# Bringing node columns by hand in a graph layer: 26 double groups on two queues, not 43 on three

## The chip, the core and the metric

The kernel runs on one core of a Trainium2 chip. The metric is device time in microseconds. Three runs of the kernel before took 5406.4, 5420.59 and 5431.38 us, so the median is 5420.59 us. A core has five engines that run side by side, each with its own queue of instructions in program order: TensorE (PE), VectorE (DVE), ScalarE (ACT), GpSimd (POOL) and SyncE (SP), which here only issues DMAs. Within a queue nothing overtakes.

## The reference, cut to what matters

There are 12,500 nodes of 128 features and 400,000 edges, sorted by their destination.

```python
h = jnp.maximum(_layernorm(x), 0.0)
s, d = (src, dst)
m = jax.nn.relu(jnp.concatenate([h[s], h[d], ea], -1) @ w1 + b1) @ w2 + b2
agg = jax.ops.segment_sum(m, d, num_segments=12500)
gi, gh = agg @ w_ih + b_ih, h @ w_hh + b_hh
# a GRU cell of gi, gh and h, added to x
```

Each edge needs a row that depends on its source node. Sources are random, so this row has to be fetched edge by edge; this fetch is what the change is about.

## The kernel before, in words

**Tables.** A first stage computes `h`, keeps it transposed in SBUF (`hT_all`, one column of 128 features for each node) and writes `A = h @ w1a`, one 512-byte row for each node, to DRAM.

**Groups and units.** The 3,125 tiles of 128 edges are cut into 391 double groups of eight tiles (`NP`, index `k`). Each double group is two units of 512 edges (`u = 2k + h`). A fully unrolled loop runs over the 782 units. For a unit, TensorE multiplies the destination part and the edge attributes with the weights (`pre`, L599), VectorE adds the source rows (`add`, L624), ScalarE applies the ReLU into `RB` (`relu`, L630), and TensorE sums the edges of each node (`seg`, L643). In program order, the round of unit `u` holds `pre(u+3)`, `add(u+2)`, `relu(u+2)` and `seg(u)`.

**Four ways to bring the source part of a double group:**

- *Gather* (most double groups): eight indirect DMAs on POOL (L147), each bringing 128 rows of `A` into a tile `G`. There are 7 such tiles (and 4 more at the start). The gathers of a double group wait until the ReLU of the double group that used the tile before is done.
- *ScalarE by hand* (19 double groups): 1,024 copies of one column each, `hT_all` to `HE_act` (L795). TensorE then multiplies the columns with `w1a` (L610), so no `A` row and no `add` is needed.
- *VectorE by hand* (18 double groups): the same with 1,024 reductions of one column (L797) into `HE_dve`.
- *SyncE by hand* (6 double groups): 1,024 plain DMAs of one 512-byte row of `A` into the tile `G_sp` (L802), of which there is one. `add` and `relu` then run as for a gathered double group.

By hand, each column's place is a register value. 32 values are loaded at a time from the tile `at` (L789).

**Which double groups, and when.** L85 to L94 spread each engine's double groups evenly over a range of `k`; for SP the range is 20 to 381. One job at a time runs on an engine. Its steps are dealt out evenly over the units between its start and its end, and they stand in the engine's queue between the ordinary work of these units:

```python
for m, kl in order.items():
    start = 2 * JOBS0
    for k in kl:
        end = 2 * k - (8 if m == "sp" else 4)
        jobs.setdefault(start, []).append((m, k, end - start))
        start = end if m != "sp" else 2 * k + 2
```

`JOBS0` is 15, so jobs start at unit 30. An SP job for double group `k` ends 8 units before it is used, and the next starts 2 units after, when `G_sp` is free.

**What else SP's queue holds.** For every four units it issues `Ld` (two DMAs, L495, destinations, three tiles) and `L` (L486, edge attributes, three tiles). `Ld` is issued 6 rounds and `L` 5 rounds before the round of its first use (`onehot_T` on DVE, L502, and `pre` on PE), and both wait for a tile to come free. For every 14 double groups it loads `xb` (L665) and stores `out` (L734).

Of the kernel before, what the change touches and what calls it, by code (L numbers as in the profile page):

```python
# [43 lines left out]
CH = PLACE * PAIR  # L44
LOAD = 32
STEP = {"act": 4, "dve": 4, "sp": 2}
SPREAD = {"dve": 18, "act": 19, "sp": 6}
NR = 12672

H_AT = 16512  # L50
# [6 lines left out]
def tile_gnn(ctx: ExitStack, tc: tile.TileContext, x, src, srcT, dstT, dstP, eaT, eaP, w1, b1, w2T, b2,  # L57
# [26 lines left out]

    mode, order = {}, {m: [] for m in SPREAD}  # L85
    for m, n in SPREAD.items():
        lo, hi = {"dve": (JOBS0 + 3, NP - 14), "act": (JOBS0 + 11, NP - 6),
# [1015 lines left out]
```

## Time and profile before

The profiled execution took 5395.6 us. Its span, first to last instruction, is 5393.5 us, so 2.1 us lie around it; it is 0.46% below the median of the three runs. In the table, a line is that of the code, "busy" counts time in instructions, and the idle time stands before the instructions of that row.

| Row of the profile | Count | Busy us | Mean of one, ns | Idle before, us |
| --- | --- | --- | --- | --- |
| L624 DVE add into G | 676 | 460.9 | 682 | 276.9 |
| L630 ACT ReLU, from G | 676 | 424.8 | 629 | 430.9 |
| L599 PE pre | 3128 | 1369.6 | 577 | 901.4 |
| L643 PE seg | 6250 | 716.4 | 371 | 0.8 |
| L610 PE on HE_dve | 288 | 56.2 | 330 | 0.1 |
| span | | 5393.5 | | |

No engine is busy for more than 58% of the span. Register loads, register moves and DMA issues are not counted as busy, and on ACT, DVE and SP these are many. The jobs run from 340 us (first row on SP at 339.9 us) to 5249 us on SP and 5342 us on ACT.

### The profile page before, as it was taken

To read this page: it belongs to the slowest core of one execution; us is meant where nothing else is said; L and a number is where in the kernel's file an instruction comes from. 1 tells how busy PE (TensorE), PEld (TensorE's weight loads), DVE (VectorE), ACT (ScalarE), POOL (GpSimd) and SP (SyncE) were. 2 spreads that over 40 slices of the span, in tenths; PEclk is the share of its full clock that TensorE was granted. 3 is DMA by queue.
4 is the path that set the end of the run, shared out by engine and by line. 5 is a ranking of instruction groups with operands and counts; after the bars stand their busy time and mean duration, and the time that the engine had idled before them with its cause. 6 is when DMAs were issued, how large, how long until landed. Compare 5 with 4: busy or idle time off the path is not lost. (4 is left out here: it accounts for less than half of the span.)

```text
span 5393.5 us, 95106 instructions
## 1 busy us (share of the span) xinstructions
PE 3101.8 (58%) x13578; PEld 1854.8 (34%) x13578; DVE 2712.7 (50%) x22515; ACT 2718.9 (50%) x20936; POOL 2654.9 (49%) x2789
## 2 busy tenths in 40 slices
PE   2664555556555556556655555665556565556557
PEld 2542333333333323333333333333333233333334
DVE  3645545545454545455545455545454555555453
ACT  2433345555555555555555555555555555555554
POOL 5445445544555454545454555544455544544452
PEclk7775665666566666666666666666666666666667
DMA  3322122222222222222221222222222222222221
GB/s 107 90 65 63 52 58 63 62 56 56 60 59 59 60 60 55 61 57 62 56 60 52 58 61 58 61 60 56 60 58 56 59 60 58 60 58 58 57 58 44
DMA packets 157887, 325.93 MB, mean 60 GB/s; under 512 B 65057, under 2 KB 77132, under 8 KB 157255
## 3 DMA queue, kind: packets, MB, share of 16 engines
q0 software_dynamic: 88992, 182.43, 13.1%
q1 hardware_dynamic: 68119, 137.33, 8.9%
q14 instruction: 520, 4.26, 0.3%
q8 instruction: 112, 1.84, 0.1%
q10 hardware_dynamic: 144, 0.07, 0.0%
HBM read 305.74 MB, written 13.84 MB: 59 GB/s over the span
## 5 line engine op out<-in xcount | busy, mean ns | idle before, releaser
L147 POOL DMA_INDIRECT G<-A,src_i x2704 | 2581.1, 955 | 2658.2 <-ACT RB L630 1766.9
L795 ACT COPY HE_act<-hT_all 128x4 uint8 x19456 | 2155.6, 189 | 1758.6 <-issue 1733.5
L797 DVE TENSOR_REDUCE HE_dve<-hT_all 128x4 uint8 x18432 | 1406.9, 146 | 1166.2 <-issue 1157.3
L599 PE MATMUL pre<-RW,L 128*128 128x256 f32 x3128 | 1369.6, 577 | 901.4 <-DVE G L624 748.7
L599 PEld LDWEIGHTS pre<-RW,L 128*128 128x128 f32 x3128 | 799.3, 282 | 1279.6 <-issue 651.5
L524 PE MATMUL oh<-w1b,hw 128*64 128x128 f32 x782 | 245.4, 412 | 1203.9 <-DVE hw L521 599.5
L643 PE MATMUL seg<-RB,OH 128*32 128x129 f32 x6250 | 716.4, 371 | 0.8 <-issue 0.8
L630 ACT ACTIVATE RB<-G 128x512 f32<-128x512 f32 x676 | 424.8, 629 | 430.9 <-issue 175.0
L533 DVE TENSOR_TENSOR RW<-oh,b1b 32x128 f32<-32x128 f32 x782 | 218.6, 279 | 773.5 <-issue 657.3
L624 DVE TENSOR_TENSOR G<-pre,G 128x512 f32<-128x512 f32 x676 | 460.9, 682 | 276.9 <-issue 269.0
L524 PEld LDWEIGHTS oh<-w1b,hw 128*64 128x64 f32 x782 | 103.6, 188 | 1416.5 <-DVE hw L521 705.7
L643 PEld LDWEIGHTS seg<-RB,OH 128*32 128x32 f32 x6250 | 382.6, 141 | 281.1 <-issue 184.8
L651 DVE COPY sums<-seg 64x128 f32<-64x128 f32 x391 | 107.4, 275 | 181.6 <-remote 94.6
L502 DVE TENSOR_SCALAR L<-Ld,node_of 64x512 f32<-64x512 int32 x391 | 192.3, 492 | 2.1 <-issue 1.6
L652 ACT CAST dcol<-seg 64x1 f16<-64x1 f32 x391 | 59.4, 152 | 232.4 <-DVE sums L651 146.0
L551 DVE TENSOR_TENSOR OH<-dloc,iota 128x256 f32<-128x256 f16 (+1 forms) x392 | 163.0, 416 | 15.2 <-issue 11.7
L674 PEld LDWEIGHTS nd<-spot,sums 64*128 64x128 f32 x782 | 160.6, 314 | 15.5 <-issue 15.5
L674 PE MATMUL nd<-spot,sums 64*128 64x40 f32 x782 | 164.6, 398 | 2.2 <-issue 2.2
L638 PE MATMUL seg<-zrow 1*64 1x129 bf16 x391 | 115.0, 294 | 0.0
L327 PE MATMUL pre<-w1a,hT_all 128*128 128x128 f32 x196 | 51.6, 414 | 77.2 <-remote 30.4
L693 PE MATMUL nd<-DEG,brow 33*128 33x512 f32 x112 | 89.4, 889 | 2.7 <-ACT RB L630 1.7
L697 PE MATMUL nd<-TOT,w2ih 128*128 128x512 f32 x112 | 87.8, 878 | 0.0
(151 smaller groups left out, 1625.5 us busy)
## 6 DMA issues: line engine op xcount, KB each, us to landing
G_sp<-A SPq DMA_DIRECT2D x6144, 0.5 KB
Ld<-in_dstP SPq DMA_DIRECT2D x390, 128.0 KB
L<-in_eaP SPq DMA_DIRECT2D x195, 256.0 KB
G<-A,src_i POOLq DMA_INDIRECT x2704
xb<-in_x SPq DMA_DIRECT2D x28, 256.0 KB
out<-xb SPq DMA_DIRECT2D x28, 256.0 KB
xs<-in_x SPq DMA_DIRECT2D x11, 512.0 KB
A<-asb SPq DMA_DIRECT2D x11, 512.0 KB
```

Source lines behind the costliest of these rows:

```text
L147: nc.gpsimd.indirect_dma_start(out=G[k][:, j, a, :], out_offset=None, in_=table, in_offset=bass.IndirectOffsetOnAxis(ap=src_i[c][:, i:i + ...
L502: nc.vector.tensor_scalar(Ls[k // QP][:2 * V, c], Ds[k // QP][:, c], node_of[:, k:k + 1], None, op0=ALU.is_equal)
L524: nc.tensor.matmul(PB_[k][:2 * V, :D], hw.rearrange("p a v -> p (a v)"), w1b, start=True, stop=True)
L533: nc.vector.tensor_tensor(RW[k % 4][s, a, :], pm[s, :D], b1b[s, :], op=ALU.add)
L551: nc.vector.tensor_tensor(o, d.to_broadcast(shape), i.to_broadcast(shape), op=ALU.is_equal)
L599: nc.tensor.matmul(PP[u][:, 2 * i:2 * i + 2, :], Ls[k // QP][:, c0:c0 + 128], RW[k % 4], start=True, stop=not raw)
L624: nc.vector.tensor_tensor(RT[u], PP.pop(u), RT[u], op=ALU.add)
L630: nc.scalar.activation(o[:, :, :D], RT.pop(u), AF.Relu)
L643: nc.tensor.matmul(SEG[k][V * a:V * (a + 1), :D + 1], OH[k][:, j, a, :], RB[u % 3][:, (j % 2) * 2 + a, :D + 1], start=False, stop=all(b != ...
L674: nc.tensor.matmul(pt[:, bass.ds(offs[i], V + SHIFT)], sums[:, i, :], spot, start=False, stop=i == n - 1)
L795: nc.scalar.copy(he[:, e * 4:e * 4 + 4], h_bytes[:, bass.ds(v - H_AT, 4)])
L797: nc.vector.tensor_reduce(he[:, e * 4:e * 4 + 4], h_bytes[:, bass.ds(v - H_AT, 4), None], AX.X, ALU.max)
```

## The change

One line: VectorE brings no columns, ScalarE brings 19 double groups as before, and SP brings 7 instead of 6.

```diff
 STEP = {"act": 4, "dve": 4, "sp": 2}
-SPREAD = {"dve": 18, "act": 19, "sp": 6}
+SPREAD = {"dve": 0, "act": 19, "sp": 7}
```

What follows from it in the queues: 18,432 reductions and their 576 register loads leave VectorE. 1,024 row DMAs and 32 register loads are added to SP, whose double groups are now 71, 123, 174, 226, 277, 329 and 381. The number of double groups that are gathered rises by 17, so POOL issues 2,840 gathers from `A` and not 2,704. For these 17 and the one on SP, VectorE's `add` takes the place of TensorE's products with `w1a` (L610). ScalarE's jobs stay as they are.

## The prediction

> **What bounds the kernel now.** I read the page's engine rows first. No engine is near full:
>
> ```profile
> PE 3101.8 (58%) x13578; PEld 1854.8 (34%) x13578; DVE 2712.7 (50%) x22515; ACT 2718.9 (50%) x20936; POOL 2654.9 (49%) x2789
> L147 POOL DMA_INDIRECT G<-A,src_i x2704 | 2581.1, 955 | 2658.2 <-ACT RB L630 1766.9
> L795 ACT COPY HE_act<-hT_all 128x4 uint8 x19456 | 2155.6, 189 | 1758.6 <-issue 1733.5
> L797 DVE TENSOR_REDUCE HE_dve<-hT_all 128x4 uint8 x18432 | 1406.9, 146 | 1166.2 <-issue 1157.3
> ```
>
> In the groups, POOL waits for ScalarE's ReLU (it frees `G`), and ScalarE and VectorE idle at "issue": their own queue is late. So I read timelines, start and length in us first. POOL in one cycle:
>
> ```profile
> 2517.96 0.94 POOL L147 DMA_INDIRECT G<-A,src_i  x1 [0.30 <-issue]
> 2519.21 0.94 POOL L147 DMA_INDIRECT G<-A,src_i  x1 [0.30 <-issue]
> 2520.45 0.94 POOL L147 DMA_INDIRECT G<-A,src_i  x1 [0.30 <-issue]
> 2524.74 0.94 POOL L147 DMA_INDIRECT G<-A,src_i  x1 [3.34 <-ACT RB L630]
> ```
>
> and ScalarE beside it:
>
> ```profile
> 2520.12 0.19 ACT L795 COPY HE_act<-hT_all 128x4 uint8 x1 [0.51 <-issue]
> 2520.83 0.19 ACT L795 COPY HE_act<-hT_all 128x4 uint8 x1 [0.52 <-issue]
> 2521.54 0.19 ACT L795 COPY HE_act<-hT_all 128x4 uint8 x1 [0.52 <-issue]
> 2522.26 0.19 ACT L795 COPY HE_act<-hT_all 128x4 uint8 x1 [0.52 <-issue]
> 2522.96 0.57 ACT L795 COPY HE_act<-hT_all 128x4 uint8 x5 [0.51 <-issue]
> ```
>
> Eight gathers follow each other at 1.25 us. In their later part ScalarE issues one column per 0.71 us; afterwards one per 0.095 us. SP's records step at the same moments, even for register moves. Over the 314 bursts of eight, ScalarE's spacing is 0.10 to 0.14 us in the first 4 us and 0.51 to 0.68 us from 7 to 11 us; it recovers 11.4 us after the burst's start. I call this the **crawl**. A cycle has a median of 14.4 us; it is crawl plus the work of the queues between crawls.
>
> Then I read SP. Its waits inside its fourth job (2876 to 3616 us; us in total, times, longest), and a piece of its timeline there:
>
> ```profile
> SPq L802 <- DMA G_sp<-A: 9.4, 20, 0.7
> SPq L802 <- DMA L<-in_eaP: 1.3, 2, 0.7
> SPq L103 <- DMA G<-A,src_i: 1.1, 1, 1.1
> ```
>
> ```profile
> 2909.68 0.83 SPq L495 DMA_DIRECT2D Ld<-in_dstP  x2
> 2910.61 0.48 SPq L486 DMA_DIRECT2D L<-in_eaP  x1
> 2911.19 14.45 SPq L802 DMA_DIRECT2D G_sp<-A  x20
> ```
>
> Against some 15 us of waits in 740 us, SP issues all the time. Twenty rows take 6.85 us outside the crawl and 14.45 us here. In this job SP loses three units against the ReLUs; in the other five it waits 23 to 81 us a job, mostly for `Ld` and `L` tiles to come free. Nobody waits for SP yet. SP is thus the queue that has no room left, and the change gives it 1,024 rows more.
>
> **The change, part by part.** Sums are made against the span of 5393.5 us.
>
> *VectorE's columns leave:* 18,432 reductions, 1406.9 us busy and 1157.3 us of issue idle, 2,564 us of its queue. What it can give is what others wait for VectorE: ScalarE's semaphore waits over 0.3 us sum to 705 us between 340 and 5340 us, half of it (276 of 560 us counted from 600 to 5000 us) in the 3 us after a crawl, where VectorE clears its columns ahead of `add`. I take at most 705 us, at least nothing, and nothing is taken unless ScalarE paces.
>
> *TensorE's L610 products:* 56 us busy, beside idle time: nothing. *36 more `add`s:* 36 x 0.682 = 25 us on VectorE, which has just lost 2,564: nothing.
>
> *17 more double groups gathered:* 136 x 1.25 = 170 us of POOL, which idles 2,658: nothing there. But 17 bursts more crawl. A double group without a burst passes in some 9 us, one with it in 14.4, so the crawl costs up to 17 x 5.4 = 92 us if everything stays on this cycle, and 0 if another queue paces that doesn't lose. Inside SP's sum it is counted below.
>
> Here the Trainium skill speaks against these rows: "SBUF — State Buffer" (SBUF: two separate sides) has engines and DMA disjoint, and only VectorE locking out GpSimd's descriptors. By it, 17 more bursts cost the other queues 0, and a silent VectorE could only speed the gathers up. The rows: a gather takes 944 ns in the median, and 945 on average in the prologue, where no column runs; and ScalarE's columns, which are no DMA, step at 0.71 us. I take the rows: no faster gather, and a crawl per burst.
>
> *SP's seventh double group.* "DMA: Bandwidth & Descriptors" (Issuing engines are not separate DMA queues) says that an issuer's time is usually small beside the DMA. By that rule this part costs about 0: DMA engines are at 22%. The row says the issue is the price: 0.323 us a row outside the crawl, 592/1024 = 0.578 us in job 4. A job now:
> - Job 4 took 741 us: 592 on rows, 149 on the rest (32 register loads at 2.1 us = 67; `L`, `Ld`, `xb`, `out` 82). Rows beyond 1024 x 0.323 = 331 are crawl: 261 us over 392 gathers, 0.666 us a gather. Jobs 2, 3, 5 and 6, waits taken off, come to 709 to 732 us; the mean of jobs 2 to 6 is 722.
> - After, jobs stand 51.6 double groups apart, so a job has 93 units of program, not 109: the rest falls by 12 us. SP may slip until 8 more ReLUs are done than its place in the program says: there PE stops at `pre` for `L`. It starts level with the ReLUs at 2k+2 and ends 2.5 units ahead of the next such point, so 100.7 of the 103.2 units of a period pass during the job, with 46.8 bursts or 374 gathers; 18 fewer x 0.666 = 12 us.
> - J = 741 - 24 = 717 us from job 4; 722 - 23 = 699 from the mean.
> - Would a silent VectorE loosen the crawl for SP? Sorting 274 bursts by VectorE's instructions in them, SP loses 58.6% of the burst in the fifth with 35 and 55.6% in that with 56: no. Around 5305 us, with SP and VectorE silent, ScalarE gets about two per step. Bounds 0 and 10% of 236 us; I take 2%, 5 us, the sorted row being nearer. J = 708 - 5 = 703 us.
>
> The other queues could pass the 103.2 units of a period in about 6.1 us each (6.81 now, less 0.96 of ScalarE's waits, plus the new bursts), 630 us, which J is above. So SP slips by its 8 units and then **sets the pace**: PE waits at `pre` for `L` (behind it stand `seg` and the next products, and ScalarE waits for them), or VectorE at L502 for `Ld` (behind it stands `add`). The DMA engines, 22% busy, don't notice 0.5 MB more.
>
> Sum: start 340; seven jobs 7J = 4921; the first has 11 units more, 32; six gaps of 2.5 units (`add`, ReLU, then `G_sp` is free), 6 x 16 = 96; from the last row, about ReLU 761, to the end 88 (the span's last 124 us after ReLU 754, less seven units at 5.2). 340 + 4921 + 32 + 96 + 88 = 5477 us, 84 us more than 5393.5. On the median of the runs, which is 27 us above the span, that is **5505 us.** J = 691 would be break-even: 0.541 us a row, against 0.553 in J = 703.
>
> **Rivals** (on the same basis).
> - *The crawl is shared more than I think.* Without VectorE, SP loses 10 to 15% less: J 667 to 693, 5250 to 5435. For it: the stretch at 5305 us; against it: the sorted bursts.
> - *ScalarE paces, faster.* VectorE was the late engine, seen in ScalarE's waits. 5393.5 - 705 + 17 bursts x 5 = 4774, on the median 4800, or 5150 if half of the waits stay. It decides only if SP keeps up at 630 us a period, 0.48 us a row; jobs 2 to 6 never went below 0.547.
> - *The gather cycle paces.* SP's slip stays covered and each double group keeps its 14.4 or 9 us: 5393.5 + 92 + 27 = 5513. Same side; it differs in that no `pre` waits for `L`.
> - *The change does less than it says*: excluded, the instruction lists have 2,840 gathers, 7,168 rows and no reduction.
>
> **Chances.** SP paces as summed, 5420 to 5600: 0.58. Shared crawl: 0.23. ScalarE paces: 0.07. Gather cycle: 0.08. Slower than 5600: 0.04. Of the first, 0.05 lies within 0.5% of the median (5393 to 5448, about what a measurement tells from no change) and 0.53 above; of the second 0.08 within, 0.15 faster. Faster 0.22, same 0.13, slower 0.65. The range leaves out ScalarE and the outermost of the others: 5300 to 5640. The likeliest alone: 5420 to 5600.
>
> **What would show it.** Right: SP issues in its jobs without waits, `L` and `Ld` come late (PE `pre` and DVE L502 wait for their DMA), ScalarE's wait turns from VectorE to those, POOL idles more. Wrong: SP still waits for tiles; rows of `G_sp` under 0.52 us; ScalarE without waits; bursts closer than 14 us.

## The result and the profile after

Five runs of the changed kernel took 5347.73 to 5369.74 us, median 5365.62; five of the kernel before took 5406.4 to 5431.38, median 5420.41. The ratio is 0.9898, 95% interval 0.9872 to 0.9925: 1.0% faster, where 1.6% slower was forecast. The profiled execution took 5347.73 us, its span is 5345.6 us.

The page's engine row and the groups that answer to those of before (busy us, mean ns of one, idle before, releaser of most of it):

```profile
PE 2754.2 (52%) x13290; PEld 1648.9 (31%) x13290; DVE 1475.8 (28%) x4119; ACT 2696.9 (50%) x20936; POOL 2781.1 (52%) x2925
L147 POOL DMA_INDIRECT G<-A,src_i x2840 | 2707.4, 953 | 2481.8 <-ACT RB L630 1524.6
L795 ACT COPY HE_act<-hT_all 128x4 uint8 x19456 | 2151.6, 189 | 1589.4 <-issue 1562.2
L599 PE MATMUL pre<-RW,L 128*128 128x256 f32 x3128 | 1226.0, 526 | 1663.6 <-DMA L<-in_eaP 1375.5
```

The last row is the one that changed its meaning. TensorE's `pre` used to wait for VectorE's `add` (748.7 us). It now waits 1375.5 us for `L`, a transfer that SP issues. SP's own waits inside its fourth job (2489 to 3171 us; total, times, longest) and a piece of its timeline there:

```profile
SPq L802 <- DMA G_sp<-A: 15.9, 31, 1.4
SPq L802 <- ACT RB L630: 9.7, 1, 9.7
SPq L486 <- PE oh L524: 0.4, 1, 0.4
```

```profile
2497.03 0.83 SPq L495 DMA_DIRECT2D Ld<-in_dstP  x2
2497.95 0.49 SPq L486 DMA_DIRECT2D L<-in_eaP  x1
2498.55 28.75 SPq L802 DMA_DIRECT2D G_sp<-A  x44
```

SP waits 26 us in 682 and issues without a pause; 44 rows with their register loads hold `L` and `Ld` back for 28.75 us. So SP sets the pace, as forecast. POOL and ScalarE in one cycle:

```profile
2517.72 0.94 POOL L147 DMA_INDIRECT G<-A,src_i  x1 [0.30 <-issue]
2518.97 0.94 POOL L147 DMA_INDIRECT G<-A,src_i  x1 [0.31 <-issue]
2530.86 0.94 POOL L147 DMA_INDIRECT G<-A,src_i  x1 [10.95 <-ACT RB L630]
```

```profile
2505.40 0.19 ACT L795 COPY HE_act<-hT_all 128x4 uint8 x1 [0.44 <-issue]
2506.11 0.29 ACT L795 COPY HE_act<-hT_all 128x4 uint8 x2 [0.52 <-issue]
2506.84 0.19 ACT L795 COPY HE_act<-hT_all 128x4 uint8 x1 [0.44 <-issue]
2507.55 0.29 ACT L795 COPY HE_act<-hT_all 128x4 uint8 x2 [0.51 <-issue]
```

The crawl's step is still 0.71 us, but before it carried one copy of ScalarE in the lines shown, and now it carries one or two. The forecast had no such change in it. The sum with the terms as they came out, from the starts of the instructions (us):

| Term | Forecast | Measured |
| --- | --- | --- |
| start | 340 | 343.7 |
| first job | 735 | 744.8 |
| six later jobs | 4218 (703 each) | 4075.5 (674 to 686, mean 679) |
| six gaps | 96 | 89.9 |
| last row to the end | 88 | 91.7 |
| span | 5477 | 5345.6 |

Four terms are off by 10 us or less. The later jobs are 142 us shorter than forecast, and the whole miss of the span is 131. A row took 0.535 us in the mean (0.531 to 0.540), where 0.553 stood in the forecast and 0.541 would have been break-even.

### The profile page after: what moved, and what is told of

It is laid out like the page before. It is cut to its first block, busy times and chain, and to the rows that moved or that the text cites. A ratio compares the mean times of both kernels' runs of the same rounds, so it can differ in the third digit from the quotient of the medians.

```text
span 5345.6 us, 77966 instructions
## 1 busy us (share of the span) xinstructions
PE 2754.2 (52%) x13290; PEld 1648.9 (31%) x13290; DVE 1475.8 (28%) x4119; ACT 2696.9 (50%) x20936; POOL 2781.1 (52%) x2925
## 5 line engine op out<-in xcount | busy, mean ns | idle before, releaser
L147 POOL DMA_INDIRECT G<-A,src_i x2840 | 2707.4, 953 | 2481.8 <-ACT RB L630 1524.6
L599 PE MATMUL pre<-RW,L 128*128 128x256 f32 x3128 | 1226.0, 526 | 1663.6 <-DMA L<-in_eaP 1375.5
L599 PEld LDWEIGHTS pre<-RW,L 128*128 128x128 f32 x3128 | 731.0, 258 | 2006.9 <-issue 1798.7
L643 PE MATMUL seg<-RB,OH 128*32 128x129 f32 x6250 | 649.4, 343 | 134.0 <-ACT RB L630 126.5
L643 PEld LDWEIGHTS seg<-RB,OH 128*32 128x32 f32 x6250 | 352.1, 131 | 401.9 <-issue 163.0
L524 PE MATMUL oh<-w1b,hw 128*64 128x128 f32 x782 | 207.1, 355 | 515.0 <-DVE hw L521 395.0
L502 DVE TENSOR_SCALAR L<-Ld,node_of 64x512 f32<-64x512 int32 x391 | 187.5, 480 | 0.0
L674 PE MATMUL nd<-spot,sums 64*128 64x40 f32 x782 | 129.8, 339 | 5.3 <-issue 5.3
L674 PEld LDWEIGHTS nd<-spot,sums 64*128 64x128 f32 x782 | 125.9, 251 | 20.7 <-issue 20.7
L521 DVE COPY hw<-hT_all 128x64 f32 x391 | 81.5, 208 | 17.3 <-issue 9.6
L147 POOL DMA_INDIRECT G<-in_x,src_i x77 | 72.8, 945 | 25.0 <-issue 23.2
```

The costliest lines, as they stand in the source:

```text
L147: nc.gpsimd.indirect_dma_start(out=G[k][:, j, a, :], out_offset=None, in_=table, in_offset=bass.IndirectOffsetOnAxis(ap=src_i[c][:, i:i + ...
L502: nc.vector.tensor_scalar(Ls[k // QP][:2 * V, c], Ds[k // QP][:, c], node_of[:, k:k + 1], None, op0=ALU.is_equal)
L524: nc.tensor.matmul(PB_[k][:2 * V, :D], hw.rearrange("p a v -> p (a v)"), w1b, start=True, stop=True)
L599: nc.tensor.matmul(PP[u][:, 2 * i:2 * i + 2, :], Ls[k // QP][:, c0:c0 + 128], RW[k % 4], start=True, stop=not raw)
L643: nc.tensor.matmul(SEG[k][V * a:V * (a + 1), :D + 1], OH[k][:, j, a, :], RB[u % 3][:, (j % 2) * 2 + a, :D + 1], start=False, stop=all(b != ...
L674: nc.tensor.matmul(pt[:, bass.ds(offs[i], V + SHIFT)], sums[:, i, :], spot, start=False, stop=i == n - 1)
```

## The experiments

All of them set the three shares (`dve`, `act`, `sp`) and nothing else unless a diff shows more. The 18 runs met two conditions. In 13 runs the kernel before, timed beside them, took 3642 to 3658 us; in 5 runs it took 5390 to 5426, much as in the result above. The traces show what differs: the 0.71 us crawl. So each experiment belongs to "with" or "without the crawl". The chip's number doesn't tell which: runs on a chip numbered 6 fell on both sides.

### The same change without the crawl

The changed kernel and the kernel before, as they are.

> The changed kernel once more, beside the kernel before on the same chip. Theory (SyncE's queue sets the pace where the gathers bring the 0.71 us crawl; GpSimd's gathers set it where they don't): on a chip where before takes 5400 us, 5345 to 5390, ratio 0.99, row cost 0.53 to 0.54 us. On a chip where before takes 3650 us, SyncE's job of 1,024 rows lasts about 470 us and no longer decides; 136 more groups to gather (17 x 8) at some 1.25 us of GpSimd each cost about 100 us: 3740 to 3760, ratio 1.025 to 1.03, the opposite sign. Rival (the chips differ by a common factor): ratio 0.99 on both.

> The kernel before, for its profile on this chip. Theory: where it takes 3650 us there is no crawl (SyncE's row 0.33 us, a job near 500 us with waits in it, so SyncE has slack), and GpSimd is busy some 2,600 us, idle about 1,000, and does not run back to back as with 17 more gathered double groups. Where it takes 5400 us: row 0.55 to 0.58 us.

Measured: the change took 3751.57 us against 3648.84, ratio 1.0292 (1.0273 to 1.0311). **The sign is the opposite.** SP's jobs 2 to 7 lasted 469 to 473 us. The changed kernel here, first its engine row, gather group and chain of waits (by engine), then a piece of SP's timeline to set beside the one above:

```profile
PE 2613.2 (70%) x13290; PEld 1596.3 (43%) x13290; DVE 1512.9 (40%) x4119; ACT 2514.5 (67%) x20936; POOL 2808.0 (75%) x2925
...
POOL 43%; issue 20%; DMA 13%; SPq 7%; PE 6%; ACT 5%; DVE 2%; ACTq 0%; POOLq 0%; DVEq 0%
...
L147 POOL DMA_INDIRECT G<-A,src_i x2840 | 2734.3, 963 | 877.9 <-issue 789.5
```

```profile
1705.73 20.26 SPq L802 DMA_DIRECT2D G_sp<-A  x44
```

Forty-four rows take 20.26 us and not 28.75. A gather takes as long as with the crawl (963 and 953 ns), but costs SP 0.03 us and not 0.58. POOL's idle time is nearly all the 0.3 us between two gathers: it runs back to back and the chain goes through it. In the kernel before, POOL was idle 904.6 us around fewer gathers, and 744.2 of it was this pause; the 160 us of other waits are 88 after the change. The rival of a common factor falls, since the sign differs.

### VectorE's 18 double groups back, everything else as changed

```diff
-SPREAD = {"dve": 0, "act": 19, "sp": 7}
+SPREAD = {"dve": 18, "act": 19, "sp": 7}
```

> VectorE's 18 double groups beside the changed kernel's orders of ScalarE and SyncE. With the crawl: theory (VectorE's issues make SyncE's rows dearer) 0.55 to 0.58 us a row and 5450 to 5600; rival (the row follows the gathers alone) 0.53 us and 5300 to 5400. Without the crawl: 3730 to 3745.

> VectorE keeps its 18 double groups, SyncE gets the seventh: SP's part of the change alone. Theory (SP paces, and VectorE's columns make its rows dearer in the crawl): a row costs 0.555 to 0.58 us, a job 700 to 717 us, time 5450 to 5600 us, PE waits for L over 1000 us. Rival (VectorE's columns never mattered to SP; the cost of the crawl was mis-sized from a job that was only unlucky): a row 0.53 to 0.54 us as in the changed kernel, job some 680 us, time 5330 to 5400 us. Rival 2 (VectorE or ScalarE paces here): SP waits for tiles, PE doesn't wait for L, time 5300 to 5420 us.

> VectorE brings its 18 double groups again, the orders of ScalarE and SyncE are the changed kernel's. Theory (a silent VectorE leaves SyncE more of the crawl): where before takes 5400 us, SyncE's row is dearer than the changed kernel's 0.535 us, 0.55 to 0.58, and the time 5450 to 5600. Rival (SyncE's row depends on the gathers alone, of which this kernel has fewer): row 0.53 us, 5300 to 5400, no slower than the changed kernel. Where before takes 3650 us: 3730 to 3745 as before, level with the changed kernel or up to 15 us below it.

> VectorE's 18 double groups beside the changed kernel's orders of ScalarE and SyncE, once more for the chip with the crawl: there theory (VectorE's issues make SyncE's rows dearer) says row 0.55 to 0.58 us and 5450 to 5600; rival (row follows the gathers alone) 0.53 us and 5300 to 5400. Without the crawl 3730 to 3745, SyncE's seven jobs of 470 us and their gaps of 16 setting the pace.

With the crawl: 5513.72 us (one execution; before 5401.29 beside it), in the theory's range of 5450 to 5600 and outside the rival's. Without: 3736.4, 3735.36 and 3741.33 us, ratios 1.025 (1.0227 to 1.0273) and 1.0237 (1.022 to 1.0254) for the first two.

Two rows of the waits of this kernel with the crawl (total, times, longest):

```profile
PE pre L599 <- DVE G L624: 696.9, 196, 7.0
...
PE pre L599 <- DMA L<-in_eaP: 305.0, 40, 14.3
```

TensorE stops for VectorE again, and for SP's `L` 40 times and not 115. SP itself is as busy as in the changed kernel, but slower. From the starts of its rows, in jobs after the first:

| With the crawl | Job us | Gathers in it | Row us | Loss per gather, us |
| --- | --- | --- | --- | --- |
| before (18, 19, 6) | 748 | 391 | 0.560 | 0.621 |
| 18, 19, 7 | 700 | 357 | 0.551 | 0.654 |
| changed (0, 19, 7) | 679 | 377 | 0.535 | 0.576 |
| 0, 19, 6 | 749 | 439 | 0.582 | 0.604 |

The loss is the rows' time beyond 0.323 us each, divided by the gathers. Between the second line and the third only VectorE's columns differ (and the gathers that replace them). There are 20 gathers more in a job, and still it is 21 us shorter: a gather costs SP 12% less (0.576/0.654), and even the whole loss of a job falls, from 233 to 217 us. The two traces are not alone in this. With SP at six double groups, reckoned in the same way, the loss per gather is 0.668 and 0.666 us with 16 double groups on VectorE (`v16_s6`, `v16_s6_b`), 0.643 with 10 (`v10_s6`) and 0.604 with none. Only before, with 18, stands outside this order with 0.621; there SP also waits for tiles, 23 to 81 us in most jobs, so its figure is not like for like. The spans differ by 5511.9 - 5345.6 = 166 us: 127 in six jobs, 48 in the gaps, 10 given back in the first job.

What a step of the crawl lets through fits this. I counted steps between 1100 and 5000 us: starts of SP, ScalarE, VectorE and TensorE's weight loads (register loads and moves too) that lie within 0.2 us, with no start in the 0.35 us before and the next start 0.5 to 0.85 us after the first. Mean number in a step:

| With the crawl | Steps | us | SP | ScalarE | VectorE | TensorE | Sum |
| --- | --- | --- | --- | --- | --- | --- | --- |
| before | 697 | 0.694 | 1.01 | 1.00 | 0.51 | 0.23 | 2.75 |
| 18, 19, 7 | 742 | 0.694 | 1.08 | 0.99 | 0.49 | 0.23 | 2.79 |
| changed | 943 | 0.700 | 1.29 | 1.25 | 0.02 | 0.15 | 2.71 |
| 0, 19, 6 | 1078 | 0.703 | 1.22 | 1.28 | 0.03 | 0.13 | 2.66 |
| 10, 19, 6 | 944 | 0.703 | 1.10 | 1.13 | 0.20 | 0.14 | 2.57 |
| 16, 19, 6 | 951 | 0.700 | 1.02 | 1.12 | 0.72 | 0.15 | 3.02 |

By and large, the fewer instructions of VectorE stand in a step, the more of SP do. That looks like a share-out of some 2.7 instructions a step, but it is no fixed quota: the last two lines have 2.57 and 3.02, and single steps of every kernel here hold from 1 to 8. What makes the step, and what sets how much it lets through, no run shows.

### Without SP's seventh double group

```diff
-SPREAD = {"dve": 0, "act": 19, "sp": 7}
+SPREAD = {"dve": 0, "act": 19, "sp": 6}
```

> The change without SyncE's seventh double group: 0, 19 and 6. With the crawl: SyncE's jobs are a sixth longer in units (118 by program and slip), so each holds a sixth more bursts; theory: 331 + 140 + 53 bursts x 8 x 0.576 = 715 us a job, six of them with gaps of 16 and 430 for start and end: 4800 to 4900. Rival: the gathers' cycle, 14.4 us with a burst, paces near 5480. Without the crawl: 3755 to 3770.

> VectorE's part alone: its 18 double groups are gathered, SP keeps six. Theory (SP paced the changed kernel): SP's job is spread over 60 double groups instead of 52, SP work of some 700 us a job against 120 units; the time falls to the next queue, 4800 to 5150 us, and PE's wait for L falls below 600 us. Rival (the gather cycle paces: every double group that is gathered costs 5 us more than one that is not): 5393 + 18 x 5 = 5480 us on the span, slower than before.

> One double group of SyncE's seven is gathered. Where before takes 5400 us: theory (SyncE paces, 7 jobs of 679 us) takes a whole job and its gap away, 690 to 700 us, until the next limit: 4650 at the least if nothing else binds, 4800 to 5150 with ScalarE's 19 orders next; rival (the gathers already pace as closely): 5300 to 5500. Where before takes 3650 us: 3745 to 3770, some 10 us above the changed kernel, one more double group of gathers.

With the crawl: 5100.4 us (one execution; before 5403.21): below before by 303 us, the fastest seen with the crawl. The theory's 4800 to 4900 was too low, since a job took 749 us and not 715 (439 gathers at 0.604 us, not 424 at 0.576); the wider 4800 to 5150 of the two earlier expectations held. The rival's 5480 is out. Without the crawl: 3756.74 and 3759.69 us, ratios 1.0295 (1.0277 to 1.0312) and 1.0306 (1.0289 to 1.0323). The four corners (us; "with" values come from three sittings, each with its own before of 5401 to 5420):

| | SP 6, with | SP 7, with | SP 6, without | SP 7, without |
| --- | --- | --- | --- | --- |
| VectorE 18 | 5402 | 5514 | 3648 | 3737 |
| VectorE 0 | 5100 | 5366 | 3758 | 3752 |

With the crawl, the change is two parts of opposite sign: VectorE's columns leaving is worth 300 us with six jobs on SP, and SP's seventh double group takes some 250 of them back (each run against the kernel before beside it). Without the crawl each part alone costs about 100 us, and both together no more. The likely reason is that one limit hides the other: with VectorE's columns and seven jobs, SP's queue is full (`v18_s7`: jobs of 468 to 478 us, gaps of 15 to 36), and without the columns POOL's gathers pace even where SP has room (`v0_s6`: gaps of 55 to 60 us).

### How many columns VectorE should bring

```diff
-SPREAD = {"dve": 18, "act": 19, "sp": 6}
+SPREAD = {"dve": 16, "act": 19, "sp": 6}
```

and in the same way 10, 19, 6 (`v10_s6`), 22, 19, 7 (`v22_s7`), 20, 21, 6 (`v20_a21_s6`) and 16, 17, 6 (`v16_a17_s6`).

> Two double groups fewer than before on VectorE alone, two more gathered. Without the crawl: if VectorE's queue sets the pace of before, the time falls until the gathers bind; these cost 10.7 us a double group (25 by hand 3759.7, 39 by hand 3607.8), so 41 by hand give 3585 to 3605. If ScalarE's queue sets the pace, no gain: 3640 to 3670. With the crawl: SyncE's row 0.55 us, 5380 to 5450.

> 16, 19 and 6 double groups once more. With the crawl as measured, 5235 to 5265, ratio 0.97. Without it, if VectorE's queue sets the pace of before there, the gathers bind next, 10.7 us a double group from 3607.8 at 39 by hand: 3585 to 3605; if ScalarE's does, 3640 to 3670.

> 10, 19 and 6. With the crawl: v16_s6 shows SyncE near its limit (jobs of 760 us, rows of 0.59 us, two or three of six gaps still slack), so theory: SyncE's six jobs of 745 to 760 us and gaps of 16 hold the time at 5050 to 5250; rival: VectorE still paces, 75 us a double group as from 18 to 16, 4800 to 4900. Without the crawl: gathers back to back, 35 by hand, 3640 to 3660.

> VectorE brings 22 double groups, four more than before; the orders of ScalarE and SyncE are the changed kernel's. With the crawl: theory (VectorE's issues make SyncE's rows dearer) 0.55 to 0.59 us a row and 5450 to 5700; rival (the row follows the gathers alone, which fall by 22 double groups) 0.51 to 0.53 us and 5200 to 5370. Without the crawl: 3730 to 3745 if SyncE's seven jobs set the pace as with 18; 3780 to 3850 if VectorE's columns do.

> Four double groups more by hand than before (20, 21 and 6, 47 in all), SyncE's share as before. Theory: on a chip without the crawl the gathers (8 of some 1.25 us a double group) and the engines' columns are near balance, so 4 fewer gathered groups bring up to 40 us: 3600 to 3650. If a column of VectorE or ScalarE costs more there than a gather of GpSimd: 3650 to 3720. On a chip with the crawl a burst less is 14 us: 5330 to 5420.

> The opposite of v20_a21_s6: two double groups fewer than before on VectorE and on ScalarE, four more gathered. Without the crawl: if the engines' columns set the pace of before (47 by hand took 3805, 155 us more), 3520 to 3600 until the gathers bind; if the gathers of GpSimd already do, 3660 to 3700. With the crawl: 4 x 8 gathers more in bursts of 8 every 14.4 us, 5430 to 5490.

With the crawl: 16 on VectorE took 5249.15 and 5236.58 us, ratios 0.9713 (0.9671 to 0.9754) and 0.9698 (0.9657 to 0.9738), where I first expected 5380 to 5450; 10 took 5208.78, ratio 0.9647 (0.9609 to 0.9684), in the theory's range. Two double groups off VectorE bring 152 to 167 us, the next six 28. SP's waits for `Ld` behind VectorE's L502 show the turn (the profile of before, then that of 16, 19, 6; total, times, longest):

```profile
SPq L495 <- DVE L L502: 289.4, 52, 24.8
```

```profile
SPq L495 <- DVE L L502: 119.3, 22, 22.5
```

In the kernel before SP's queue was full, but VectorE's held it up; with two double groups less VectorE holds it up less (the five gaps between SP's jobs sum to 176 us, before to 347), and SP is next. TensorE's `pre` shows the handover: with 18, 16, 10 and 0 double groups on VectorE it waits 749, 322, 89 and 41 us for VectorE's `add`, and 163, 394 and 485 us for SP's `L` in the last three; before has no such wait.

Without the crawl VectorE can pace too: 22 on VectorE took 4035.54 us (one execution), 297 more than 18 with the same SP and ScalarE, and above both ranges that I had given. Neither theory for 20, 21, 6 had its 3805.03 us, ratio 1.0434 (1.0415 to 1.0454). 16, 17, 6 took 3607.8, ratio 0.9891 (0.9868 to 0.9914), just outside the first of its two ranges. The chains of 22, 19, 7 and of 16, 17, 6, by engine:

```profile
DVE 42%; issue 22%; PE 10%; SPq 7%; POOL 6%; DMA 6%; DVEq 3%; ACT 2%; ACTq 0%; POOLq 0%
```

```profile
POOL 35%; issue 20%; DVE 15%; DMA 12%; PE 11%; ACT 2%; SPq 2%; DVEq 1%; ACTq 0%; POOLq 0%
```

The pace passes from VectorE to POOL between them. On which side the kernel before stands is not shown: 16, 17, 6 and 20, 21, 6 change ScalarE's share as well, and the run that would tell, 16, 19, 6, met the crawl both times. Three versions thus beat the two kernels: 0, 19, 6 (5100) and 16, 19, 6 with the crawl; 16, 17, 6 without. Only 0, 19, 6 was run on both sides, and it loses 3% without. What 16, 19, 6 does without the crawl, or 16, 17, 6 with it, was not tried.

### Three that met no crawl

`halves` cuts each gathered tile in two, so that a burst has four gathers and its own ReLU to wait for:

```diff
-        G[k] = pool.tile([128, GRP, 2, D], F32, name="G")
+        G[k] = [None, None]
...
+            G[k][u % 2] = pool.tile([128, 2, 2, D], F32, name="G")
...
-                    out=G[k][:, j, a, :], out_offset=None, in_=table,
+                    out=G[k][u % 2][:, j % 2, a, :], out_offset=None, in_=table,
```

The pools get twice as many of these smaller tiles. `v0_s0` has 0, 19 and 0 (and leaves out a fill of SP's part of a tile, which is then empty); `v0_a0_s7` has 0, 0 and 7.

> The changed kernel with each gathered tile cut into two of one unit each, so a burst is four gathers that wait for one unit's ReLU, and not eight. If the crawl sets in only after some gathers stand in GpSimd's queue together, then where before takes 5400 us the row costs some 0.40 us and the time falls to 4400 to 4900. If every gather brings the same crawl, the row stays at 0.53 to 0.54 us and the time within 5300 to 5400. Where before takes 3650 us: within 1 % of the changed kernel.

> ScalarE alone brings columns; SP and VectorE none, so 24 more double groups are gathered than before. Theory: ScalarE paces; with its two neighbours silent it gets more columns through the crawl (mean spacing 0.51 to 0.68 us late in a burst before, under 0.40 here); time 4800 to 5100 us. Rival (gather cycle): 372 gathered double groups at 14 us, over 5300 us.

> SP alone brings rows; ScalarE and VectorE bring no columns, 36 more double groups are gathered than before. If a queue's loss in the crawl depends on how many others issue, a row falls below 0.50 us and the time to 5000 to 5250 us. If it doesn't, a row stays at 0.53 to 0.54 us, SP still paces, and the time is that of the changed kernel, 5340 to 5400 us, a little more for the gathers.

`halves` took 3741.93 us, ratio 1.0263 (1.0246 to 1.028), within 1% of the changed kernel beside it; whether a shorter burst softens the crawl stays open. `v0_s0` took 3812.58, ratio 1.0449 (1.0423 to 1.0474), `v0_a0_s7` 3946.16, ratio 1.0819 (1.08 to 1.0838). They give POOL's price without the crawl: from 25 double groups by hand (3756.74) to 19 it is 9.3 us each, from 19 to 7 11.1, near the 8 x 1.25 = 10 us of the gathers. What each would do with the crawl was not seen.

## Why the prediction was wrong

**Right.** SP sets the pace: hardly a wait in its jobs (26 us of the 682 of the fourth), `pre` waits for `L`, and without the seventh job the time falls by 250 us. Start, gaps, slip, tail and the last row's place (ReLU 761) came as summed; 368 to 384 gathers in a job, 374 forecast; 127 to 134 us of a job beside its rows, 137 forecast. A gather is no faster without VectorE's columns (953 ns, 955 before). The 36 more `add`s did no harm: VectorE is busy 1475.8 us.

**The step that failed** is the one answered with "no": would a silent VectorE loosen the crawl for SP? It was taken at 2%, 5 us of a job, with 10% as the outer bound. It measured 12% a gather, and with SP at six double groups, from 16 on VectorE to none, 10% (0.604 against 0.668 us). Had VectorE's columns stayed while the gathers rose to 377, the job of 18, 19, 7 would be 700 + 20 x 0.654 = 713 us, where the sum had 708 ahead of this term; the changed kernel has 679. So the term is about 34 us a job, not 5.

**Why it looked like nothing.** The sorted bursts had 35 to 56 instructions of VectorE in them, and there the loss is flat: 58.6 to 55.6%. After the change a burst has 4 to 15. Sorted in the same way, in fifths, the changed kernel's bursts cost SP 46.6% of the burst at 4 instructions, 48.1 at 7, 51.2 at 9, 52.6 at 11 and 56.9 at 15. At 15 the loss is already near that of before; in this kernel the relief lies below, where the trace of before had 5 bursts of 285. But a sort inside one trace is no proof in this direction either. In a like count (rows' time beyond 0.323 us in the 11.5 us from a burst's first gather), 0, 19, 6 loses 53% at 5 instructions and 56% at 16, a much smaller slope, and 10, 19, 6 loses 54% at 18 and 59 to 60% from 30 up. That a queue without columns costs SP less comes from the runs set side by side; how the loss goes with the number in a burst stays open. The other observation, ScalarE with two copies a step while SP and VectorE were silent, lay in the right range, and was outvoted.

**The rival that came true** is the shared crawl: J of 667 to 693 us, 5250 to 5435 us; it had 679 and 5366. It was given 0.23 for its mechanism against 0.58.

**The rule and the row.** By the prediction's reading of the Trainium skill's "SBUF — State Buffer" (SBUF: two separate sides), 17 more bursts cost other queues nothing. That agrees with the runs without the crawl (0.03 us a gather on SP) and not with those that have it (0.58 and more). The section is about memory ports; the crawl holds up register moves too (SP's, between its rows, took 29 ns in the median and up to 1402 before), so these runs say nothing against its ports. By the same reading, "DMA: Bandwidth & Descriptors" (Issuing engines are not separate DMA queues) would price SP's 1,024 rows near 0. They cost 90 to 110 us where VectorE's columns stayed and 250 where they left with the crawl; only where they left without it did they cost nothing (3752 us, 3758 without them).

**Smaller points.** VectorE's leaving was counted at nothing on the path beside that term. It is worth 300 us when SP has six double groups. About half of that came with the first two double groups: before, VectorE held up the pace. The rest came as SP took over the pace: from 16, 19, 6 to 0, 19, 6 SP's later jobs, the gaps between them and the end grow shorter, some 137 us of the span in all. VectorE's part was in the waits (SP for `Ld` behind L502, 23 to 81 us in five of six jobs) and in the rival of ScalarE's waits, whose 4800 to 5150 us is where 0, 19, 6 landed. "POOL idles more" was wrong: 2481.8 us after, 2658.2 before. The cycle between two bursts fell from 14.4 to 13.4 us, which the forecast had named as a sign against it.

## What to carry to other kernels

A relation sorted out of one trace holds for the range that the trace covers: if the change takes a quantity from 50 to 5, bursts with 35 to 56 say nothing of it, and the few that lie near the new value weigh more than the many that don't. A run beside it settles what the sort can't. Take a change with two parts apart, one run each: here they were worth -300 and +250 us. And time a balance of shares where it will run: the same edit is 1.0% faster with the crawl and 2.9% slower without it.

## What the runs showed of the hardware

**The crawl is not always there.** The same kernel takes 5400 us with it and 3648 without. GpSimd's gathers and ScalarE's copies take about as long in both (after the change 953 and 963 ns, 189 and 189); TensorE's products are longer with it (`pre` 526 ns at a mean granted clock of 0.68, 499 at 0.76). It needs no job by hand: in the prologue, where 77 gathers from `in_x` follow each other, the windows of the changed kernel with the crawl, then without (columns: window, its length, busy us and count of PE, PEld, DVE, ACT and POOL, clock, DMA share, GB/s):

```profile
20.00:40.00 20.00, 0.00 (x0) 0.00 (x0) 1.65 (x9) 0.85 (x3) 15.12 (x17) 1.00 0.36 89
```

```profile
20.00:40.00 20.00, 18.89 (x91) 18.12 (x91) 19.49 (x88) 13.14 (x33) 15.12 (x17) 1.00 0.76 264
```

POOL does the same 17 gathers in both; the other engines run 12 instructions in one and 303 in the other, at a granted clock of 1.00 in both, so a throttled TensorE is not the cause. The start is 120 us longer (first row on SP at 343.7 and 224.3 us). Nor are DMA packets much slower: those of POOL's queue took 133 ns in the mean in the changed kernel with the crawl, 120 without, and 117 in 0, 19, 6 with the crawl. Whether the chip, its neighbours or something else turns it on stays open.

**A step's content.** During a crawl 2.57 to 3.02 instructions start in the mean per step of 0.69 to 0.70 us, over SP, ScalarE, VectorE and TensorE together, and SP gets more of them where VectorE has fewer.
